# A four-layer convolution and attention kernel: ScalarE issues two of the eight row gathers of v per step, and VectorE sums the two heads ahead of the residual

## The chip, the cores and the metric

The kernel runs on one core of one Trainium2 chip. The metric is the time of one execution on the device in microseconds (us); the value quoted for a kernel is the median of its runs. A core has five engines that work from instruction queues of their own: TensorE (PE, matrix products; PEld is its loading of weights), VectorE (DVE), ScalarE (ACT), GpSimd (POOL) and SyncE (SP, which here only starts DMA transfers). Each engine executes its queue in the order in which it was written; engines wait for each other by semaphores.

## The reference, cut to what matters

Four residual layers are computed on x of shape (8, 128, 56, 56), all in float32: window attention, a recurrent network, a masked convolution and a pair of 3x3 convolutions. The change touches only the first. For each of 8 images, with 7 x 7 windows of 64 pixels, 8 heads of 16 channels, and for each window the 4 windows that its mean query likes best:

```python
xn = group_norm(x)                                  # 32 groups of 4 channels
q, k, v = xn @ W_qkv + b_qkv                        # per pixel, 128 channels each
_, r_idx = top_k(q_win * 128**-0.5 @ k_win.T, 4)    # 4 of 49 windows, for each window
attn = softmax(q_h * 128**-0.5 @ k_h[r_idx].T)      # 8 heads, 64 queries x 256 keys
o = attn @ v_h[r_idx]
x = x + (o + depthwise3x3(v) + lepe_b) @ W_o + b_o
```

## The kernel before, in words

Layer 0 is a software pipeline over 196 pairs of windows (8 images x 49 windows, two at a time). One pass of its last loop is called a step here. In step `p` the engines work on several pairs at once: `gather` (L487) copies the chosen keys of pair p+3 on POOL; `fetch` (L505) starts the DMA transfers that bring the chosen rows of v of pair p+2; `scores` (L524) multiplies queries and keys of pair p+2 on PE, and `maxima` (L539, four instructions max0 to max3) takes their row maxima on DVE; `halve`, `flip` and `flipped` bring these maxima onto the right partitions (POOL, PE, ACT); `shifted` (L560) computes the transposed and shifted scores of pair p+1 on PE; `exponentials` (L583, four instructions exp0 to exp3) takes their exponentials on ACT; and `values` (L589) multiplies exponentials and rows of v of pair p on PE into the PSUM tile `po`.

The results of a head pair lie in two halves of `po`, which have to be masked and added. `first_heads` (L607) scales the first half on ACT into `v`, and `both_heads` (L612, instruction L615) adds the second half to it on DVE. `divisors` (L617) prepares the divisors on DVE, and `divide` (L633) multiplies on POOL.

Beside this a planner gives most steps one or two further jobs, called `one` and `two`, each a product on PE and an ending (`end1`, `end2`) on ACT or DVE: keys, queries, pixels or rows of v for the next image (endings on ACT), the depthwise convolution (24 matmuls, L420, ending on ACT), or `project` (L439), the output projection. The ending of `project` is the residual, L450 on DVE, which adds the projection (PSUM) to X. There are 56 of them, one per strip of 7 windows. `hooks` are small loose pieces of work, most of them statistics on DVE.

The order of the work within a step is written out by hand: two strings list the names, SHORT for most steps, LONGER for those with a depthwise convolution, and in these strings lies the order on each of PE, ACT, DVE and POOL. SP is not bound by it, but takes its transfers in the order of their making.

PSUM tiles are shared, and this ties the engines to each other. `po` lies in the same bank (s0) as a quarter of the scores: the scores of the next pair can begin only after `both_heads` has read `po`, and `values` only after max0 has read its scores. `one` uses bank t0, `two` t1 and `flip` t2, which `shifted` also writes and exp0, exp1 and exp2 read.

The rows of v lie in DRAM as `vpix`, one block of 64 pixels x 128 channels (32 KB) per window. A pair needs eight of them (2 windows x 4 chosen). They go to `ring`, which has room for 6 windows, that is three pairs. In `fetch`, ScalarE's queue issues the first (o = 0, t = 0) and SP's queue the other seven. Before `values` of a pair, PE waits on the two semaphores `landed` of its windows (L594). Which window is chosen is known only at run time: `chosen` (L474) loads the indices into registers of the issuing engine (TENSOR_LOAD at L470), for SP and POOL four windows at a time, for ScalarE the index t = 0 of every second of seven windows, so four values and one load for about four steps.

Of the kernel before, what the change touches and what calls it, by code (L numbers as in the profile page):

```python
# [26 lines left out]
NWIN = NW * NW  # L27
# [3 lines left out]
TOPK = 4  # L31
# [15 lines left out]
def conv_stack_kernel(ctx: ExitStack, tc: tile.TileContext, a: dict, out: bass.AP):  # L47
# [3 lines left out]
    nc = tc.nc  # L51
# [76 lines left out]
    with ExitStack() as l0:  # L128
# [41 lines left out]
        for i in range(2):  # L170
            t = c0.tile([P, WS, PW], F32, name=f"vrow{i}", tag=f"vrow{i}")
# [10 lines left out]
        qs, ks, selrs, v3s, lepes, os_, st1, norms = {}, {}, {}, {}, {}, {}, {}, {}  # L182
        later, tails = [], []
# [281 lines left out]
        known = {}  # L465
        landed = [tc.alloc_semaphore(f"landed{k}") for k in range(RING)]

        def loaded(src, engine):

            return nc.values_load_multi_w_load_instructions(  # L470
                src, engines=[engine], min_val=0, max_val=NWIN - 1,
                skip_runtime_bounds_check_because="indices of maxima over 49 values, clamped to 48",
            )[1]

        def chosen(W, t, engine):

            if (engine, W, t) not in known:
                b, w = divmod(W, NWIN)
                if engine == mybir.EngineType.Activation:
                    at = selrs[b].rearrange("p (w t) -> p w t", t=TOPK)[:, w : min(w + 7, NWIN) : 2, t]  # L480
                    known.update(((engine, W + 2 * k, t), v) for k, v in enumerate(loaded(at, engine)))
                else:
                    vs = loaded(selrs[b][0:1, w * TOPK : min(w + 4, NWIN) * TOPK], engine)
                    known.update(((engine, W + k // TOPK, k % TOPK), v) for k, v in enumerate(vs))
            return known[engine, W, t]

        def gather(W):  # L487


            for W in (W, W + 1):  # L490
                b, w = divmod(W, NWIN)
                i, j = divmod(w, NW)
                kw = win.tile([P, TOPK, WPX], F32, name=f"ks_{W}", tag="ks", bufs=5)
                for t in range(TOPK):
                    at = chosen(W, t, mybir.EngineType.Pool)
                    nc.gpsimd.tensor_copy(kw[:, t : t + 1, :], ks[b][:, bass.ds(at, 1), :])  # L496
                qm = win.tile([P, 2, WPX], F32, name=f"qm_{W}", tag="qm", bufs=5)
                nc.gpsimd.tensor_tensor(
                    qm, qs[b, i][:, j : j + 1, :].broadcast_to((P, 2, WPX)),
                    hmask.rearrange("p (h o) -> p h o", o=1).broadcast_to((P, 2, WPX)), ALU.mult,  # L500
                )
                wins[W] = dict(kw=kw.rearrange("p t x -> p (t x)"), qm=qm)

        def section(W, c):
            return 4 * (W % RING) + 2 * c + 1  # L505

        def fetch(W):

            for o in range(2):
                for t in range(TOPK):  # L510
                    h = (t % 2) * WPX
                    engine, kind = (nc.sync, mybir.EngineType.SP) if o or t else (
                        nc.scalar, mybir.EngineType.Activation)
                    at = chosen(W + o, t, kind)
                    dma = engine.dma_start(
                        ring[h : h + WPX, section(W + o, t // 2), :],
                        vpix[(W + o) // NWIN][bass.ds(at, 1)].rearrange("o x c -> (o x) c"),
                    )
                    dma.then_inc(landed[(W + o) % RING], 16)
                    tc.no_tile_sem_insts.add(dma.ins.name)  # L520
                    tc.add_to_no_dep_group(f"rows{W + o}", dma.ins)
# [33 lines left out]
        def flipped(p):  # L555
            t = pairs[p]["nm"] = win.tile([P, 2, P], BF16, name=f"nm_{p}", tag="nm", bufs=1)
            nc.scalar.copy(t, pairs[p]["flip"])
# [54 lines left out]
        def both_heads(p):  # L612

            s_ = pairs[p]
            nc.vector.scalar_tensor_tensor(s_["v"], s_["po"][:, :, 1], hmask[:, 1:2], s_["v"], ALU.mult, ALU.add)  # L615

        def divisors(p):  # L617


            s_ = pairs[p]  # L620
            t = win.tile([P, 2, 2, 2, CL], F32, name=f"den_{p}", tag="den", bufs=1)
            nc.vector.transpose(
                t.rearrange("p o h b r -> p (o h b r)"), s_["po"].rearrange("p o h q -> p (o h q)")
            )
            at = t[:, 0, 0, 0, 16:17]
            den = bass.AP(at.tensor, at.offset, [list(at.ap[0]), [4 * CL, 2], [CL, 2], [2 * CL - 16, 2]])
            rden = win.tile([P, 2, 2, 2, 1], F32, name=f"rden_{p}", tag="rden", bufs=1)
            nc.vector.reciprocal(rden.rearrange("p o b h c -> p o b (h c)"), den)
            s_["d"] = win.tile([P, 2, WPX], F32, name=f"d_{p}", tag="d", bufs=1)
            nc.vector.transpose(  # L630
                s_["d"].rearrange("p o (k r) -> p (o k) r", r=CL),
                rden.rearrange("p o b h c -> p (o b) h c").broadcast_to((P, 4, 2, 16)),
            )  # L633

        def divide(p):

            s_ = pairs.pop(p)
            for o in range(2):
                W = 2 * p + o
                b, w = divmod(W, NWIN)  # L640
                i, j = divmod(w, NW)
                if j == 0:
                    os_[b, i] = strip.tile([P, WS, HW], F32, name=f"o_{b}_{i}", tag="o")
                n = 2 if o == 0 and j + 1 < NW else 1
                if o == 1 and j > 0:
                    continue
                dst = os_[b, i][:, :, j * WS : (j + n) * WS]
                nc.gpsimd.tensor_tensor(
                    dst.rearrange("p u (o v) -> p o u v", v=WS),
                    s_["v"][:, o : o + n].rearrange("p o (u v) -> p o u v", v=WS),  # L650
                    s_["d"][:, o : o + n].rearrange("p o (u v) -> p o u v", v=WS), ALU.mult,
                )
# [12 lines left out]
        made, jobs, hooks, fixed, loose = {}, [], {}, [], []  # L665
# [14 lines left out]
        def pair_of(b, w):  # L680
            return (b * NWIN + w) // 2
# [40 lines left out]
        for f in (image[0], image[1], *pixels[1:]):  # L722
# [3 lines left out]
                     light=(ps_s, "s2"), tails=(ps_s, "s1"))  # L726
# [19 lines left out]
        for b in range(1, B):  # L746

            at = [FIRST + 1] * NBLK if b == 1 else [pair_of(b - 2, 0) + 2 * i - 1 for i in range(NBLK)]
# [9 lines left out]
            at = [pair_of(b - 1, i * NW) - 5 for i in range(NBLK)]  # L758
            if b == 1:
                at = [max(t, 4 + 3 * i // 2) for i, t in enumerate(at)]  # L760
# [16 lines left out]
        for p in range(FIRST, END + 6):  # L777
            ready = [t for t in jobs if t[1] <= p and all(placed.get(k, p) < p for k in t[7])]
            light, long = (next((t for t in ready if t[5] == k), None) for k in (LIGHT, LONG))
            ready = [t for t in ready if t[5] == ONE]  # L780
            one = next((t for t in ready if not t[4]), None)
            if long:
                one, two = one if len(ready) > (MANY if p > 20 else 8) else None, long
# [3 lines left out]
            if light and two and two[4] and p < light[0]:  # L787
                light = None
# [9 lines left out]
        for b, i in itertools.product(range(B), range(NBLK)):  # L798
            p = placed["project", b, i]
# [5 lines left out]
        for lo, hi, n, f in sorted(loose, key=lambda t: t[0]):  # L805
            p = min(range(lo, min(hi, END + 5) + 1), key=lambda p: (weight[p], p))
# [21 lines left out]
        for k, (name, n) in enumerate(VECTORS):  # L828
# [4 lines left out]


        SHORT = """fetch scores shifted gather max0 max1 values exp0 max2 exp1 max3 halve ahead one light two flip exp2
            divisors first end1 exp3 flipped both divide lit hooks tails end2"""
        LONGER = """fetch scores shifted gather max0 max1 values exp0 max2 exp1 max3 halve ahead two exp2 divisors first
            flip light one exp3 flipped both divide lit hooks tails end2 end1"""

        def ahead(p):  # L840
            for W in (2 * p - 2, 2 * p - 1):
# [19 lines left out]
        for p in range(FIRST, END + 6):  # L861
            one, two, light = (t and t[3]() for t in plan[p])
# [3 lines left out]
            if 0 <= p + 2 < END:  # L866
                acts.update(scores=lambda: scores(p + 2), halve=lambda: halve(p + 2), flip=lambda: flip(p + 2),
                            flipped=lambda: flipped(p + 2))
# [6 lines left out]
            if 0 <= p < END:  # L875
                acts.update(values=lambda: values(p), first=lambda: (first_heads(p), root_table(p)),
                            both=lambda: both_heads(p), divisors=lambda: divisors(p), divide=lambda: divide(p))
            if p >= 0 and p + 2 < END:
                acts["fetch"] = lambda: fetch(2 * p + 4)
# [13 lines left out]
            for W in (0, 2) if p == -1 else ():  # L893
                fetch(W)
# [11 lines left out]
    with ExitStack() as l1:  # L906
# [5 lines left out]
        at = np.cumsum([0] + [n for _, n in VECTORS])  # L912
# [18 lines left out]
        t = c1.tile([P, B], F32, name="t1")  # L931
# [154 lines left out]
        with tc.manual_schedule(engines={mybir.EngineType.PE}):  # L1086
# [3 lines left out]
            for s in range(0, END, 2):  # L1090
# [22 lines left out]
                if s + 2 == WARM:  # L1113
                    first = [row.tile([P, 2, 2, NCH, B], F32, name=f"first{f}", tag=f"hs{f}", bufs=3) for f in range(2)]
# [10 lines left out]
        known = st2[:, : len(tiles), :]  # L1125
# [762 lines left out]
```

## Time and profile before

| | us |
|---|---|
| median of 3 timed runs | 3370.28 (3366.54 to 3371.79) |
| the profiled execution, whole | 3365.47 |
| its span, first to last instruction | 3363.6 |
| TensorE busy in it | 3246.4 (97%) |
| VectorE busy | 1767.8 (53%) |
| ScalarE busy | 1412.6 (42%) |
| GpSimd busy | 1291.8 (38%) |

Layer 0 covers about the first 1190 us: the 196 steps are marked by the 196 transposes of `divisors` (L622), the first at 50.9 us and the last at 1187.9 us. In a row of the timeline the first number is the start, the second the duration, both in us; then come engine, line, operation, tiles (written, then read), shapes and a count; in brackets stands how long the engine had been idle before it and what ended that. "SPq" and "ACTq" are the queues of SP and ScalarE when they issue a transfer, which does not count as busy time. The granted clock of TensorE was 0.988 over the span.

### The profile page before, as it was taken

How to read it: one execution, taken by the hardware profiler on the slowest of the kernel's cores; microseconds unless marked ns; L12 is line 12 of the kernel's file. 1: busy time of each engine (PE TensorE's matmuls, PEld its weight loads, DVE VectorE, ACT ScalarE, POOL GpSimd, SP SyncE). 2: the span in 40 equal slices, each digit the busy share in tenths (PEclk: the TensorE clock that was granted, in tenths of full speed). 3: DMA queues.
4: the chain of work that ended last, by engine and by line, in shares of the span. 5: the costliest groups of instructions: out<-in, count | busy, mean ns of one | idle time of the engine just before them, and what ended most of it. 6: DMA issues, size and time to landing. Idle time of an engine off the chain costs nothing.

```text
span 3363.6 us, 103407 instructions
## 1 busy us (share of the span) xinstructions
PE 3246.4 (97%) x41152; PEld 2743.4 (82%) x41152; DVE 1767.8 (53%) x4066; ACT 1412.6 (42%) x2935; POOL 1291.8 (38%) x3797
## 2 busy tenths in 40 slices
PE   7999999999999899999999999999999999999998
PEld 5777767667676689999999999999999953489898
DVE  5888888788776732221111111111122247799999
ACT  4666666566665522222222222222211144455554
POOL 4777877877777721111111111111000046422221
PEclk9999999999999989999999999999999999999999
DMA  5455555545445411110000000000012146301001
GB/s 152 132 142 134 146 142 134 138 124 143 124 129 140 112 58 45 48 48 18 1 1 1 1 1 1 1 1 1 1 51 60 57 122 181 94 20 39 27 32 40
DMA packets 197564, 239.02 MB, mean 71 GB/s; under 512 B 42848, under 2 KB 150112, under 8 KB 197072
## 3 DMA queue, kind: packets, MB, share of 16 engines
q0 software_dynamic: 34624, 117.03, 12.7%
q1 hardware_dynamic: 145936, 108.38, 11.3%
q10 hardware_dynamic: 16512, 6.90, 0.9%
q8 instruction: 326, 5.34, 0.7%
q14 instruction: 166, 1.36, 0.1%
HBM read 133.64 MB, written 67.56 MB: 60 GB/s over the span
## 4 chain that ended last, share of the span: by engine, by line
PE 75%; DVE 18%; issue 3%; POOL 1%; ACT 1%; DMA 1%; SPq 0%; POOLq 0%; DVEq 0%; ACTq 0%
PE ps L1041 35%; PE s L534 6%; PE po L600 6%; PE po L1076 5%; PE plep L420 4%; PE pc L1267 4%; PE t L576 4%; DVE nmax L541 3%; PE pi L1016 3%; PE t L566 1%; PE pc L1275 1%; DVE u_pc3b L1632 1%; PE pq L390 1%; PE pvp L319 1%; DVE va L1499 1%
## 5 line engine op out<-in xcount | busy, mean ns | idle before, releaser
L1041 PE MATMUL ps<-hs,w_gates 128*128 128x136 f32 x7680 | 932.9, 280 | 0.4 <-issue 0.4
L1041 PEld LDWEIGHTS ps<-hs,w_gates 128*128 128x128 f32 x7680 | 911.1, 190 | 8.6 <-issue 0.5
L1064 ACT ACTIVATE hs<-ps,bg 128x136 f32<-128x136 f32 x744 | 237.9, 371 | 933.1 <-PE ps L1041 925.6
L586 ACT ACTIVATE e<-t 128x512 f32<-128x512 f32 x784 | 445.6, 595 | 345.3 <-PE t L576 273.6
L541 DVE TENSOR_REDUCE nmax<-s 128x2 f32<-128x512 f32 x784 | 487.0, 685 | 196.4 <-PE s L534 195.6
L1019 DVE SCALAR_TENSOR_TENSOR inp<-pi,bine,th 128x272 f32<-128x272 f32 x186 | 84.7, 496 | 889.2 <-ACT th L1018 889.2
L1005 POOL TENSOR_TENSOR xn<-X,ctr 128x136 f32<-128x136 f32 (+1 forms) x186 | 96.3, 536 | 876.4 <-PE pi L1016 871.6
L1041 PEld LDWEIGHTS ps<-inp,w_gates 128*128 128x128 f32 x2976 | 370.2, 190 | 13.5 <-PE pi L1016 1.1
L1041 PE MATMUL ps<-inp,w_gates 128*128 128x136 f32 x2976 | 375.4, 279 | 0.7 <-PE pi L1016 0.7
L496 POOL COPY ks<-kT 128x64 f32 x1568 | 297.0, 234 | 106.2 <-PE t L576 64.8
L600 PE MATMUL po<-e,ring 128*32 128x64 f32 x12544 | 247.2, 231 | 24.7 <-DVE nmax L541 17.9
L600 PEld LDWEIGHTS po<-e,ring 128*32 128x32 f32 x12544 | 220.0, 149 | 49.6 <-DVE nmax L541 20.1
L534 PE MATMUL s<-ks,qm 32*128 32x256 f32 x3136 | 228.4, 403 | 19.0 <-DVE v L615 15.2
L576 PE MATMUL t<-qm,ks 32*128 32x128 f32 x6272 | 235.6, 273 | 0.6 <-issue 0.6
L576 PEld LDWEIGHTS t<-qm,ks 32*128 32x128 f32 x6272 | 216.5, 188 | 4.8 <-issue 1.4
L1513 PE MATMUL pc3b<-vb,u_w2c_t 128*128 128x196 f32 x1152 | 200.9, 336 | 19.9 <-DVE vb L1494 19.9
L1513 PEld LDWEIGHTS pc3b<-vb,u_w2c_t 128*128 128x128 f32 x1152 | 197.3, 194 | 22.2 <-DVE vb L1494 22.0
L1076 PE MATMUL po<-hs,xw 128*128 128x272 f32 x744 | 203.9, 396 | 3.4
L1513 PE MATMUL pc3a<-va,u_w1c_t 128*128 128x196 f32 x1152 | 198.2, 332 | 9.1 <-DVE d_pc3a L1530 4.3
L1513 PEld LDWEIGHTS pc3a<-va,u_w1c_t 128*128 128x128 f32 x1152 | 192.9, 191 | 13.6 <-issue 10.2
L534 PEld LDWEIGHTS s<-ks,qm 32*128 32x128 f32 x3136 | 144.6, 185 | 50.1 <-DVE v L615 27.4
L1076 PEld LDWEIGHTS po<-hs,xw 128*128 128x128 f32 x744 | 132.0, 190 | 28.8 <-ACT hs L1068 9.1
(288 smaller groups left out, 4410.7 us busy)
## 6 DMA issues: line engine op xcount, KB each, us to landing
ring<-vpix SPq DMA_DIRECT2D x1372, 32.0 KB
v<-vimg POOLq DMA_DIRECT2D x56, 290.0 KB, 3.9
v<-vimg POOLq DMA_DIRECT2D x56, 289.5 KB, 4.8
v<-vimg POOLq DMA_DIRECT2D x56, 289.0 KB, 5.7
kept<-gk SPq DMA_DIRECT2D x56, 272.0 KB, 2.0
g<-kept SPq DMA_DIRECT2D x56, 272.0 KB, 2.6
xkeep<-X POOLq DMA_DIRECT2D x56, 224.0 KB, 2.5
vimg<-vrow POOLq DMA_DIRECT2D x54, 232.0 KB, 2.8
```

Of the source, the lines that this page charges most:

```text
L420: nc.tensor.matmul(st["pl"][g * CL : (g + 1) * CL], wlep[:, dy, g, :], rows[:, g, dy : dy + WS, :HW], start=(dy == 0), stop=(dy == 2),)
L496: nc.gpsimd.tensor_copy(kw[:, t : t + 1, :], ks[b][:, bass.ds(at, 1), :])
L534: nc.tensor.matmul(s_["s"][g][:, o, :], w["qm"][h].rearrange("p h x -> p (h x)"), w["kw"][h], start=True, stop=True,)
L541: nc.vector.tensor_reduce(s_["nmax"][:, :, g], s_["s"][g], AX.X, ALU.max, negate=True)
L576: nc.tensor.matmul(s_["t"][g][:, o, c], w["kw"][h, c * P : (c + 1) * P], w["qm"][h].rearrange("p h x -> p (h x)"), start=False, stop=(o == ...
L586: nc.scalar.activation(s_["e"][g], s_["t"][g], AF.Exp)
L600: mm = nc.tensor.matmul(po[g * CL : (g + 1) * CL, o, h], flat[:, at : at + 8 * CL - 7 : 8], s_["e"][g][:, o, c, h * WPX : (h + 1) * WPX], ...
L1041: nc.tensor.matmul(ps[f][:, i], w, src, start=(i == 0 and k == 0 and h != fresh), stop=(k == KH - 1 if h else k == KI - 1 and (s < WARM or ...
L1064: nc.scalar.activation(hs[f][:, s % 2, i], ps[f][:, i], AF.Tanh, bias=bg[:, m : m + 1])
L1076: nc.tensor.matmul(po, wout[:, k, :], hs[k // 2][:, :, k % 2], start=(k == 0), stop=(k == KH - 1))
L1267: nc.tensor.matmul(pcs[n][r * CL : (r + 1) * CL], w3[:, dy, r, :], rows3[:, r, i * WS + dy : i * WS + dy + WS, :HW], start=(dy == 0), stop ...
L1513: nc.tensor.matmul(bank[:, half].rearrange("p (y x) -> p y x", x=H4), u[:, dy, k, :], v[:, k, i * RB + dy : i * RB + dy + RB, :], start=(d ...
```

## The change

In `fetch` ScalarE issues the gather t = 0 of both windows of a pair, so two, and SP six. For that ScalarE's load takes the index t = 0 of eight windows in a row in place of every second of seven. In both lists of names `both` moves: in SHORT to between `first` and `end1`, ahead of the residual where `one` is a projection; in LONGER to right behind `first`, where nothing of DVE stands between the old and the new place except for the endings that follow later anyway.

```diff
@@ chosen
                 if engine == mybir.EngineType.Activation:
-                    at = selrs[b].rearrange("p (w t) -> p w t", t=TOPK)[:, w : min(w + 7, NWIN) : 2, t]
-                    known.update(((engine, W + 2 * k, t), v) for k, v in enumerate(loaded(at, engine)))
+                    at = selrs[b].rearrange("p (w t) -> p w t", t=TOPK)[:, w : min(w + 8, NWIN), t]
+                    known.update(((engine, W + k, t), v) for k, v in enumerate(loaded(at, engine)))
@@ fetch
-                    engine, kind = (nc.sync, mybir.EngineType.SP) if o or t else (
+                    engine, kind = (nc.sync, mybir.EngineType.SP) if t else (
                         nc.scalar, mybir.EngineType.Activation)
@@ the order of a step
         SHORT = """fetch scores shifted gather max0 max1 values exp0 max2 exp1 max3 halve ahead one light two flip exp2
-            divisors first end1 exp3 flipped both divide lit hooks tails end2"""
+            divisors first both end1 exp3 flipped divide lit hooks tails end2"""
         LONGER = """fetch scores shifted gather max0 max1 values exp0 max2 exp1 max3 halve ahead two exp2 divisors first
-            flip light one exp3 flipped both divide lit hooks tails end2 end1"""
+            both flip light one exp3 flipped divide lit hooks tails end2 end1"""
```

## The prediction

> **What bounds the kernel now.** I read the page for the share of each engine, then the views of one line (L622, L515) for the rhythm, then the waits of PE, then the timeline of three stretches. Layer 0 is the only part that the change touches.
>
> ```profile
> PE 3246.4 (97%) x41152; PEld 2743.4 (82%) x41152; DVE 1767.8 (53%) x4066; ACT 1412.6 (42%) x2935; POOL 1291.8 (38%) x3797
> ```
> ```profile
> L622 DVE STREAM_TRANSPOSE den<-po x196: 427/450/452, 50.9 to 1187.9; 128x256 f32<-128x256 f32 x196
> ```
> ```profile
> L515 SPq DMA_DIRECT2D ring<-vpix x1372: 468/468/1777, 32.9 to 1183.0; - x196
> L515 ACTq DMA_DIRECT2D ring<-vpix x196: 476/482/548, 44.7 to 1172.3; - x196
> ```
> ```profile
> 164.69 139.22 SPq L515 DMA_DIRECT2D ring<-vpix  x168
> ```
>
> PE is the engine that is nearly always busy. The 196 marks of L622 lie (1187.9 - 50.9) / 195 = 5.83 us apart: that is a step. A second queue has no air either: SP issued 168 gathers, the share of 24 steps, in 139.22 us, or 5.80 us a step, without a pause in the timeline. An issue takes 468 ns, but with its register work and the index loads between them they follow at 0.83 us, and some take up to 1777 ns. SP starts about three pairs ahead and loses this lead: counted in the trace, from SP's last issue for a pair to PE's use of the pair 10 to 15 us pass in the first ten steps and 2 to 5 us in the last fifteen. So two things are near the limit: PE with what it waits for, and SP.
>
> ```profile
> PE s L534 <- DVE v L615: 15.0, 41, 1.0
> ...
> PE po L600 <- DMA ring<-vpix: 4.1, 1, 4.1
> ```
> ```profile
> 1049.38 0.31 DVE L630 STREAM_TRANSPOSE d<-rden 128x128 f32<-128x128 f32 x1
> ...
> 1049.61 0.65 DVE L450 SCALAR_TENSOR_TENSOR X<-py,bo,X 128x448 f32<-128x448 f32 x1
> ...
> 1050.04 0.28 PE L553 MATMUL flip<-ident,halves 128*128 128x128 bf16 x2
> ...
> 1050.17 0.34 DVE L615 SCALAR_TENSOR_TENSOR v<-po,hmask,v 128x128 f32<-128x128 f32 x1
> ...
> 1050.57 1.15 PE L534 MATMUL s<-ks,qm 32*128 32x256 f32 x16 [0.26 <-DVE v L615]
> ...
> 1056.96 1.30 PE L600 MATMUL po<-e,ring 128*32 128x64 f32 x40 [4.13 <-DMA ring<-vpix]
> ```
>
> This is a step with a residual. PE is through with the flip at 1050.32 and stands 0.26 us, because the scores need the PSUM bank that L615 has yet to read, and L615 stood behind the residual. The last line is PE waiting 4.13 us for gathered rows.
>
> **The change part by part.**
>
> (1) *The sum ahead of the residual.* Before, L615 starts 0.56 us after L450 (1049.61 to 1050.17). Without L450 ahead it starts where L450 starts now, its inputs being there (the halves of ScalarE end 0.1 to 0.2 us before the divisors in nearly all steps). Nothing else on DVE moves; behind L615 wait L450 and the hooks, and they end when they end now. What PE gets depends on its own work, by classes counted over the trace:
> - 20 steps with the projection and an image row (L301) as second job: PE idles 0.27 us on average; the next exp0 has 0.22 us to spare against ScalarE's ending of that job. Gain 0.225 x 20 = 4.5.
> - 7 with the projection and queries (L390): 0.26 idle, 0.27 to spare. 0.25 x 7 = 1.75.
> - 12 with pixels (L319): 0.12 idle. 0.12 x 12 = 1.4.
> - 5 with the projection alone: about 1.0 idle; the scores can start 0.57 earlier. 0.57 x 5 = 2.85.
> - Of the rest some 0.3 in all; where a depthwise convolution is beside it, nothing moves on DVE.
>
> Sum 10.8 us. What is late next: L450 ends 0.3 us later against the scores, while `shifted`, which overwrites its PSUM bank, comes 0.97 us after the start of the scores and the residual needs 0.31 + 0.65 from the same point: it just fits. Max0 has DVE idle for 0.3 to 1.2 us before it in these steps, more than the scores come earlier. Without this cover the 10.8 shrink towards 0.
>
> (2) *One gather less on SP.* Six at 0.83 are 4.97 us in a step of 5.83, so the lead is kept. Then the stalls on rows go: 4.13 us (above) and, in the last fifteen steps, where PE starts 0.13 us after the landing, 0.25 + 0.34 + 0.23 + 1.52 = 2.3 us. Sum 6.4. It is also what lets part (1) count: at 5.80 of 5.83 a faster PE would only wait for SP. On SP everything behind the moved gather comes earlier, with one exception: by the order of the changed program both weight loads for layer 1 (1.0 and 0.5 MB) now stand directly ahead of the same pair's gathers that stalled; before, one of them stood a pair earlier.
>
> (3) *One gather more on ScalarE.* It stands at the head of the step, ahead of exp0 to exp3; for them wait PE's jobs (through the banks), `first_heads`, the flip's copy and the ending of `two`, which PE's `shifted` needs.
>
> ```profile
> 805.23 0.52 ACTq L515 DMA_DIRECT2D ring<-vpix  x1
> ...
> 805.99 1.09 ACT L586 ACTIVATE e<-t 128x512 f32<-128x512 f32 x2 [1.25 <-PE t L576]
> ...
> 809.46 0.48 ACTq L515 DMA_DIRECT2D ring<-vpix  x1
> 809.57 0.61 ACT L338 COPY vp<-pvp 128x512 f32<-128x512 f32 x1
> ...
> 811.42 1.09 ACT L586 ACTIVATE e<-t 128x512 f32<-128x512 f32 x2 [1.25 <-PE t L576]
> ```
>
> A further gather costs about 0.65 us of the queue: at the start three of them take 1.86. The second case is the ordinary one: the issue ends at 809.94, exp0 starts when PE releases it at 811.42, and 1.48 us lie between; 0.65 of it costs nothing. The first is a step with an index load (median 920 ns) ahead of the gather: 0.24 us lie between. Counted over the trace 42 steps have less than 0.65, and their shortfalls add up to 16.8 us with the usual 0.05 between issue and exp0. That is the upper bound of the cost; the lower is 0. Of each shortfall the 0.24 us that exp2 waits for `values` anyway swallow a part; with a depthwise convolution next, exp1 has 0.15 to spare, and the idle time before the flip's copy (0.4 to 1.2) takes more. Step by step that leaves 2.0 in ordinary steps, 2.2 in residual steps and 1.9 in those with the convolution: I take 6.1. The new loads (56 for 52) shift by one step for every second image, to like places.
>
> (4) *The beginning.* The first pair's second gather now waits for ScalarE, which issues it 0.65 us after the first (44.66, 45.3), while SP had issued it by 37.5. PE waits for exactly this landing at 48.87. Cost 0.65.
>
> Sum: -10.8 - 6.4 + 6.1 + 0.65 = -10.5 us. The profiled execution took 3365.47 (span 3363.6 and 1.9 around it), so 3355.0 by its measure. It stands 4.8 under the median of the runs, 3370.28; measured like that median the forecast is 3359.8.
>
> A rule that speaks against this: the Trainium skill, "DMA: Bandwidth & Descriptors", section "Issuing engines are not separate DMA queues", says that transfers started from several engines share the same 16 DMA engines, and that this only saves sequencer time, usually little beside the transfer. By it the 6.4 us of part (2) would stay, and the sum would be -4.1. The row on SP says that here sequencer time is what has run out, while the DMA engines are busy about half the time (share 0.52 from 100 to 300 us): by it the sum is -10.5.
>
> **The rivals.**
> - *ScalarE's lateness eats the gain* (0.15). For: the 42 tight steps; in 104 steps the flip's copy has idle time before it, in the rest none. Against: the spare times in (3). With all 16.8: -17.2 + 16.8 + 0.65 = +0.3, so 3370.5.
> - *The rows land late all the same* (0.10), because the transfers collide (gathers landing 4 to 5 us after their issue occur where 870 KB for the convolution or the layer 1 weights are under way). Then (2) gives nothing: -4.1, so 3366.2. This is also the case in which that half of the change does not do what it says.
> - *More than I count* (0.12). ScalarE's lateness is swallowed whole: -16.6, so 3353.7.
> - *Slower* (0.13). The second issue on ScalarE, right behind the first, is not 0.48 us long but slow, as SP's are when several are under way (up to 1.78; 8% of them over 1.0). In the 50 steps with an index load there is no cover left, so each 0.1 us of it costs 5 us; from 0.2 us it has eaten the gain, from 0.34 the kernel is measurably slower. With 0.5: +25 - 10.5 = +14.5, so 3384.8. Against: ScalarE's own issues never took over 0.55, but then it had one at a time.
>
> **How the numbers follow.** Forecast -10.5: 3359.8, chance 0.50, own range 3355.7 to 3363.5 (ScalarE's cost 2 to 10 in place of 6.1). 0.2% is 6.7 us, about what a measurement of this kernel can tell from no change; the bound lies at 3363.5. Faster: forecast and "more than I count", 0.62. Within: the first two rivals, 0.25. Slower: 0.13. The range for 8 in 10 goes from 3351 (just under the 3353.7) to 3374 (the first two rivals, and a second issue slow by up to a quarter us); beyond it I leave the rest of the slower case and a little below.
>
> **What would show it.** In the changed profile: L615 ahead of L450 in the residual steps, and the wait of scores on L615 down from 15.0 us to about 3; SP's gathers at 1176 with pauses between groups of six; no wait of L600 on the ring behind the first step; ScalarE's issues at 392, of 0.48 us each; exp0 late by up to 0.6 us every fourth step and in no others; the marks of L622 about 10 us closer in all. I am wrong if exp0 comes late in ordinary steps too, if the pair behind the weight loads still stalls by 4 us, or if the waits on L615 turn into equal ones on L450 (by `shifted`) or on max0 (by `values`).

## The result

The changed kernel is slower. Its median is 3389.43 us (3380.94 to 3393.65, 6 runs), that of the kernel before on the same chip 3368.41 us (3362.79 to 3371.79, 6 runs): a ratio of 1.0063, with an interval from 1.0047 to 1.008, or 21 us more. The forecast was 3359.8, with a range of 3351 to 3374: wrong in sign, and outside the range.

### The profile page after: what moved, and what is told of

The parts are those of the page before. It is cut to its first block, busy times and chain, and to the rows that moved or that the text cites. A ratio compares the mean times of both kernels' runs of the same rounds, so it can differ in the third digit from the quotient of the medians.

```text
span 3391.6 us, 103411 instructions
## 1 busy us (share of the span) xinstructions
PE 3249.3 (96%) x41152; PEld 2737.9 (81%) x41152; DVE 1776.9 (52%) x4066; ACT 1400.1 (41%) x2935; POOL 1292.9 (38%) x3797
## 4 chain that ended last, share of the span: by engine, by line
PE 76%; DVE 14%; issue 4%; ACT 2%; ACTq 2%; POOL 1%; DMA 1%; SPq 0%; DVEq 0%; POOLq 0%
PE ps L1041 35%; PE po L1076 5%; PE po L600 5%; PE s L534 5%; PE plep L420 4%; PE t L576 4%; PE pc L1267 4%; PE pi L1016 3%; PE t L566 2%; PE py L445 1%; ACTq L515 1%; PE pq L390 1%; PE pvp L319 1%; PE pc L1275 1%; PE pc3b L1513 1%
## 5 line engine op out<-in xcount | busy, mean ns | idle before, releaser
L586 ACT ACTIVATE e<-t 128x512 f32<-128x512 f32 x784 | 441.2, 596 | 377.5 <-PE t L576 203.2
L600 PE MATMUL po<-e,ring 128*32 128x64 f32 x12544 | 245.5, 230 | 16.8 <-DVE nmax L541 13.3
L600 PEld LDWEIGHTS po<-e,ring 128*32 128x32 f32 x12544 | 218.4, 149 | 41.6 <-DVE nmax L541 14.9
L420 PE MATMUL plep<-v,wlep 96*32 96x448 f32 x1344 | 140.3, 550 | 20.0 <-ACT e L586 20.0
```

The source lines that it names most:

```text
L420: nc.tensor.matmul(st["pl"][g * CL : (g + 1) * CL], wlep[:, dy, g, :], rows[:, g, dy : dy + WS, :HW], start=(dy == 0), stop=(dy == 2),)
L586: nc.scalar.activation(s_["e"][g], s_["t"][g], AF.Exp)
L600: mm = nc.tensor.matmul(po[g * CL : (g + 1) * CL, o, h], flat[:, at : at + 8 * CL - 7 : 8], s_["e"][g][:, o, c, h * WPX : (h + 1) * WPX], ...
```

## The profile after

The profiled execution took 3393.65 us, with a span of 3391.6. First the shares of the engines on its page, then the rhythm of the steps (L622: count, shortest, median and longest in ns, first and last start in us).

```profile
PE 3249.3 (96%) x41152; PEld 2737.9 (81%) x41152; DVE 1776.9 (52%) x4066; ACT 1400.1 (41%) x2935; POOL 1292.9 (38%) x3797
```
```profile
L622 DVE STREAM_TRANSPOSE den<-po x196: 427/450/452, 51.6 to 1213.1; 128x256 f32<-128x256 f32 x196
```

PE has as much work as before, but the step is now (1213.1 - 51.6) / 195 = 5.96 us long instead of 5.83. So PE waits more: 25 of the 28 us by which the span grew have come by the end of layer 0. The granted clock (0.99) is no lower than before. The waits of PE between 60 and 1215 us say for whom (us in total, times, longest):

```profile
PE plep L420 <- ACT e L586: 20.0, 16, 2.3
PE po L600 <- DVE nmax L541: 13.3, 8, 2.6
PE pq L390 <- ACT e L586: 10.7, 16, 1.2
...
PE py L445 <- ACT e L586: 4.9, 8, 1.2
PE s L534 <- DVE v L615: 4.3, 12, 0.4
...
PE pvp L319 <- ACT e L586: 2.9, 7, 0.4
```

Two of the intended effects are there: the wait of the scores on L615 fell from 15.0 us to 4.3, and there is no wait of L600 on the ring any more. But four rows are new. The jobs `one` and `two` (L420, L390, L445, L319) wait for the exponentials of L586, which have yet to read the banks that the jobs write: 20.0 + 10.7 + 4.9 + 2.9 = 38.5 us. Before, these jobs waited for them 0.2 us in all. So ScalarE is late. What it does ahead of its exponentials shows in the timeline of one step:

```profile
801.03 0.38 ACT L557 COPY nm<-flip 128x256 bf16<-128x256 bf16 x1
801.15 0.48 ACTq L515 DMA_DIRECT2D ring<-vpix  x1
801.28 0.72 ACT L307 ACTIVATE vrow<-pvt,bqkv 128x448 f32<-128x448 f32 x1
...
803.27 1.24 PE L600 MATMUL po<-e,ring 128*32 128x64 f32 x64
...
803.86 0.50 ACTq L515 DMA_DIRECT2D ring<-vpix  x1
...
804.41 1.57 ACT L586 ACTIVATE e<-t 128x512 f32<-128x512 f32 x3 [2.41 <-PE po L600]
...
805.55 2.46 PE L420 MATMUL plep<-v,wlep 96*32 96x448 f32 x24 [1.04 <-ACT e L586]
```

ScalarE's first gather is issued by 801.63, the second only at 803.86. Between them the timeline shows nothing for ScalarE, because a load into registers does not count as work; in the trace it stands there from 801.66 to 803.67. Exp0 should start where `values` (L600) starts, at 803.27. It starts at 804.41, right behind the second gather and 1.14 us late, and L420 waits 1.04 us for the exponentials. The bracket behind L586 names PE as what ended the idle time; that is only the last event the profile knows of. In the trace it lies at 804.04, and the last product of `shifted`, which exp0 reads, had ended at 803.34. What exp0 waited for stood ahead of it in its own queue.

The load has a row of its own in the view of L470 (shortest, median and longest in ns). Of the kernel before:

```profile
L470 ACTq TENSOR_LOAD <-selr x52: 284/920/1822, 43.2 to 1155.4; - x52
```
And after:
```profile
L470 SPq TENSOR_LOAD <-selr x104: 302/976/1708, 29.9 to 1201.8; - x104
L470 ACTq TENSOR_LOAD <-selr x56: 282/1733/2364, 44.6 to 1202.2; - x56
```

ScalarE's load has doubled, from 0.92 to 1.73 us, as it takes eight values where it took four. (SP takes sixteen in 0.98 us, but its sixteen are neighbours in the list, while ScalarE's are every fourth.) Counted over the trace, exp0 starts 1.16 us after the start of `values` on average in the 52 steps with a load. What goes beyond 0.05 us in a step adds up to 58.0 us; before it was 1.3 us. In the other steps nothing changed (0.9 us against 1.3).

By an account of PE over layer 0, from the first `values` to the last (1138.9 us before, 1162.8 after, so +23.9): the four waits for exponentials +39, the scores' wait on L615 -12, waits of `values` -8, idle time ahead of `flip` and `shifted` +3, the products themselves +2. The layer also starts 1.4 us later.

## Experiments

Three explanations were set against each other. **L**: the index load, now 1.73 us and with a second gather behind it, no longer fits into the time that ScalarE has ahead of exp0. **I**: the second issue of a gather on ScalarE is itself what makes it late (the last rival of the prediction). **O**: the new order of the sum harms. Each kernel is compared with the kernel before on its own chip, where that took 3377.8, 3378.9 and 3375.4 us in the three groups; a difference in us is the measured ratio applied to that time, so it can be off by 1 to 2 us from the difference of the medians. "Lateness" is the sum over the steps with a load of what exp0 starts more than 0.05 us after `values`, counted in the trace.

### The order alone

```diff
# before, with nothing but the two strings changed:
-            divisors first end1 exp3 flipped both divide lit hooks tails end2"""
+            divisors first both end1 exp3 flipped divide lit hooks tails end2"""
-            flip light one exp3 flipped both divide lit hooks tails end2 end1"""
+            both flip light one exp3 flipped divide lit hooks tails end2 end1"""
```


> Only the two lists of names are changed: the sum of the heads stands ahead of the residual, the gathers and ScalarE's index load are as before. Theory L (the changed kernel is slow because its index load on ScalarE, eight values that lie four apart, lasts 1.73 us in place of 0.9 and holds back the exponentials): nothing of that is here, so this is not slower than before. The wait of the scores on L615 falls from 15.0 us to about 4, and the time by 2 to 11 us: less than 10.8 if SP, which needs 5.80 of a step's 5.83 us, takes over as the limit; then waits for gathered rows grow. Theory O (the order itself does harm, by a residual that now comes late): slower by 5 us or more.

Measured: 3375.18 us, ratio 0.9992 [0.9981, 1.0004], no difference. PE's first waits between 60 and 1215 us:

```profile
PE po L600 <- DMA ring<-vpix: 18.4, 12, 4.2
PE po L600 <- DVE nmax L541: 15.5, 11, 2.6
PE s L534 <- DVE v L615: 4.7, 13, 0.4
```

The wait on L615 has fallen to 4.7 us, but the layer is as long as in the execution of before that was profiled later (1150.9 us both, though on different chips). By an account of PE in these two, the scores' idle time is 12 us less; about 5 us of it come back as idle time ahead of L600, where the waits on gathered rows are 18.4 us in place of 14.7, 6 us in the first products of `shifted` (see part (1) below), and the rest is spread. So SP takes back a part of the gain and `shifted` another. O falls: nothing here is slower.

### Gathers moved, with neighbouring indices

```diff
 (before's order; SP also copies the indices t = 0 of an image into a row of their own)
+                sel0s[b] = samp.tile([1, NWIN], I32, name=f"sel0_{b}", tag="sel0")
+                nc.sync.dma_start(sel0s[b], sel[:, 0:1])
...
+                    at = sel0s[b][0:1, w : min(w + 8, NWIN)]
...
-                    engine, kind = (nc.sync, mybir.EngineType.SP) if o or t else (
+                    engine, kind = (nc.sync, mybir.EngineType.SP) if t else (
```


> Only the gathers are changed: ScalarE issues two and SP six, the lists of names are as before, and ScalarE's indices come from a row of their own in which the choices t = 0 of an image's windows lie side by side (one more tiny transfer per image), so that it loads eight neighbouring values. Theory L: the load lasts about 0.5 us (SP's load of 16 neighbours lasts 0.97, of 4 neighbours 0.30), the exponentials are hardly late, and the waits for rows (6.4 us) go: 4 to 7 us faster than before. Theory I (it is the second issue on ScalarE that holds the exponentials back, whatever the load): 15 us slower or more.

Measured: 3360.36 us, ratio 0.9949 [0.9936, 0.9962], 17 us faster and more than any theory had. The load takes 0.55 us, lateness is 4.2 us. The second issues are as irregular as in the changed kernel (0.64 us on average, 21 over 1 us, the longest 2.0), and they cost nothing that can be seen. I falls.

### The whole change, with neighbouring indices

```diff
 (the changed kernel with the row of indices above)
-                    at = selrs[b].rearrange("p (w t) -> p w t", t=TOPK)[:, w : min(w + 8, NWIN), t]
+                    at = sel0s[b][0:1, w : min(w + 8, NWIN)]
```


> The whole change, with ScalarE's indices from the row of neighbouring values. Theory L: load about 0.5 us, so the whole of the gains that were forecast and little of the cost: 10 to 17 us faster than before, and the waits of PE's jobs on the exponentials (38 us in the changed kernel) gone to under 5. Theory I: 15 us slower or more than before, as the changed kernel.

Measured: 3350.01 us, ratio 0.9921 [0.9908, 0.9935], 27 us faster than before, and more than the 10 to 17 that L expected. Its load, and PE's first waits between 60 and 1215 us (its lines are numbered 3 higher):

```profile
L473 ACTq TENSOR_LOAD <-sel x56: 290/551/1099, 45.6 to 1159.0; - x56
```
```profile
PE po L603 <- DVE nmax L544: 13.9, 9, 2.7
PE s L537 <- DVE v L618: 5.3, 16, 0.5
PE flip L556 <- POOL halves L551: 3.9, 5, 1.1
```

Neither a wait for exponentials of any size nor one on the ring is left. A step with a load in the timeline, to be laid beside that of the changed kernel:

```profile
796.25 0.48 ACTq L518 DMA_DIRECT2D ring<-vpix  x1
796.36 0.59 ACT L339 COPY vp<-pvp 128x512 f32<-128x512 f32 x1
...
797.51 0.49 ACTq L518 DMA_DIRECT2D ring<-vpix  x1
...
798.20 1.09 ACT L589 ACTIVATE e<-t 128x512 f32<-128x512 f32 x2 [1.25 <-PE t L579]
```

The load (796.76 to 797.31 in the trace) stands at the same place, between the two gathers. The second gather ends at 798.00, and exp0 starts at 798.20, with `values` at 798.21: now it really is PE that releases it, with 0.2 us to spare. So one array's layout decides the sign of the whole change: 56 loads of 0.55 us instead of 1.73.

### The long load with one gather

```diff
 (before, ScalarE still issuing one gather; only the load takes all eight windows)
-                    at = selrs[b].rearrange("p (w t) -> p w t", t=TOPK)[:, w : min(w + 7, NWIN) : 2, t]
-                    known.update(((engine, W + 2 * k, t), v) for k, v in enumerate(loaded(at, engine)))
+                    at = selrs[b].rearrange("p (w t) -> p w t", t=TOPK)[:, w : min(w + 8, NWIN), t]
+                    known.update(((engine, W + k, t), v) for k, v in enumerate(loaded(at, engine)))
```


> The kernel before, with one thing of the change: ScalarE loads the indices t = 0 of eight windows in a row (four of them are not used), but still issues one gather. Theory L: the load lasts 1.73 in place of 0.9 us; of that the room before the exponentials hides about half and the wait of the third exponential 0.24 more, so some 50 steps are later by 0.2 to 0.4 us: 6 to 20 us slower than before. Theory I: no difference (within 3 us), since the second issue is not there.

Measured: 3381.71 us, ratio 1.0006 [0.9994, 1.0019], no difference: a miss for L's number, and what theory I expected (which fell with the two kernels above, and would not have with this one alone). The load is 1.83 us and lateness 22.9 us, but PE waits for exponentials only 7 us, and its waits on the ring come to 10.9 us (14.7 in the execution of before profiled below). That would fit a late PE giving time to SP, which this kernel waits for anyway; no run isolates it. What is shown is that the long load costs what it does only together with the second gather.

### The long load and both gathers, in before's order

```diff
 (the changed kernel with before's two strings)
-            divisors first both end1 exp3 flipped divide lit hooks tails end2"""
+            divisors first end1 exp3 flipped both divide lit hooks tails end2"""
```


> Before's order of the names, but the second gather on ScalarE and its index load of eight values 16 bytes apart, as in the changed kernel. My theory (the index load of 1.73 us ahead of two gathers makes exp0 late in every fourth step, some 55 us of lateness in all, of which PE waits for e about 38): slower than before by 5 to 32 us; exp0 late by 45 to 65 us in sum over the steps with a load, and PE's waits on e of L586 25 to 45 us. The rival that the new order of the sum harms, together with the load: no slower than before, with PE's waits on e below 10 us. The rival that a second gather alone is too slow for ScalarE has already fallen with the run of neighbouring indices.

Measured: 3391.51 us, ratio 1.004 [1.0025, 1.0055], 13 us slower; lateness 52.8 us, waits for exponentials 15.0 + 10.5 + 5.9 + 2.9 = 34.3 us. This half of the change carries the loss by itself.

### The changed kernel with shorter loads

```diff
 (the changed kernel; first kernel)
-                    at = selrs[b].rearrange("p (w t) -> p w t", t=TOPK)[:, w : min(w + 8, NWIN), t]
+                    at = selrs[b].rearrange("p (w t) -> p w t", t=TOPK)[:, w : min(w + 2, NWIN), t]
 (second kernel: min(w + 4, NWIN))
```


> The whole change, but ScalarE loads two indices (16 bytes apart) every second step in place of eight every eighth window: a load of about 0.45 us in place of 1.73, in nearly every step. My theory (what costs is how much longer than the room of some 1.5 us between two gathers' end and PE's release the load and the second gather together are in one step): 0.45 + 0.65 fits, so a time near that of the kernel with neighbouring indices, faster than before by 17 to 28 us; exp0's lateness below 12 us in sum. The rival that the sum of what ScalarE spends on indices counts, however it is cut (196 x 0.45 = 88 us against 56 x 1.73 = 97): slower than before by 10 to 20 us, like the changed kernel.

> The whole change with loads of four indices 16 bytes apart, in every second step: 0.9 us each, the length that the forecast gave the load. My theory: with 0.65 for the second gather and 0.05 between, 0.9 + 0.65 is just over the room of 1.48 us less what the ordinary step has spare; exp0 is late by 0.1 to 0.5 us in some 100 steps, most of it swallowed: faster than before by 10 to 24 us, between the kernel with neighbouring indices and the changed one, and nearer the former. The rival (the sum of time spent on loads): slower by 5 to 20 us, as 104 x 0.9 = 94 us are spent, as many as in the changed kernel.

Measured: with two values 3348.76 us, ratio 0.9916 [0.9901, 0.9931], 28 us faster than before; with four 3358.64 us, ratio 0.9944 [0.9929, 0.996], 19 us faster. Their loads:

```profile
L470 ACTq TENSOR_LOAD <-selr x200: 282/482/894, 44.4 to 1158.8; - x100
```
```profile
L470 ACTq TENSOR_LOAD <-selr x104: 281/894/1592, 44.5 to 1166.9; - x104
```

Added up in the traces, the 200 loads take 104 us and the 104 loads 95 us, no less than the 56 loads of the changed kernel (92 us). Still the time goes from -28 over -19 to slower than before, and lateness from 5.0 over 21.9 to 58.0 us. What counts is not the time spent on indices, but by how much a single load with its gathers is longer than the room in its step.

### Before once more, profiled

> The kernel before, profiled once more, on the same chip as the three others. If the stalls on the gathered rows are what the moved gather was worth more than 6.4 us for, PE's waits of L600 on the ring are 10 to 25 us here and not 6.4; if they are 6.4 again, the gain of the moved gather must have come from somewhere else.

Measured: 3377.64 us, with PE's first waits

```profile
PE s L534 <- DVE v L615: 15.7, 42, 1.0
PE po L600 <- DMA ring<-vpix: 14.7, 9, 3.4
```

The wait on L615 is that of the first execution, that on the ring is not: 14.7 us in nine waits instead of 4.1 in one. The layer is 12 us longer (1150.9 against 1138.9). Seen from here the 17 us of the moved gather are explained in the main, as that kernel has no such wait; they were small in the prediction because the execution it was read from had few stalls. On the chip where the moved gather was measured, before itself was timed but not profiled.

### The changed kernel once more, and the distance of the indices

```diff
 (against the whole change with neighbouring indices: the row now holds the first two choices of each window, values 8 bytes apart)
-                nc.sync.dma_start(sel0s[b], sel[:, 0:1])
+                nc.sync.dma_start(sel0s[b], sel[:, 0:2])
...
-                    at = sel0s[b][0:1, w : min(w + 8, NWIN)]
+                    at = sel0s[b].rearrange("p (w t) -> p w t", t=2)[:, w : min(w + 8, NWIN), t]
```


> The changed kernel once more, beside the repaired ones on their chip, since before took 3368 on the first chip and 3378 on the others, where it stalls more on gathered rows. The changed kernel has no such stalls, so its own time should not depend on the chip: 3381 to 3394 again, slower than before by 5 to 25 us, and at least 25 us slower than the kernel with neighbouring indices. If it were at or below before, the first comparison would have been one of chips.

> The whole change with ScalarE's eight indices 8 bytes apart (a row of the first two choices of each window) in place of 16 (the changed kernel: 1.72 us a load) or 4 (neighbours: 0.55). If a load costs some 0.21 us for each value that has no neighbour beside it in the list, 1.7 us, and a time like that of the changed kernel, +5 to +25 us against before. If it costs that much for each stretch of 16 bytes that it touches (eight values in 64 bytes, four stretches), 0.9 to 1.1 us, exp0 late by 10 to 25 us in sum, and faster than before by 10 to 24 us.

Measured: the changed kernel 3388.82 us, ratio 1.0044 [1.0027, 1.0061]; with values 8 bytes apart 3388.76 us, ratio 1.0041 [1.0027, 1.0056]. The changed kernel takes the same time on both chips, and is slower on both; what differs is before, with its stalls. The load 8 bytes apart:

```profile
L473 ACTq TENSOR_LOAD <-sel x56: 280/1732/2583, 43.0 to 1197.0; - x56
```

It takes the 1.73 us of 16 bytes apart, and lateness is the same too (57.2 us in the changed kernel, 55.2 here). Whether lone values lie 8 or 16 bytes apart doesn't matter; being neighbours does.

### A third gather on ScalarE

```diff
 (neighbouring indices, eight in every second step; ScalarE issues t = 0 of both windows and t = 1 of the first)
-                    engine, kind = (nc.sync, mybir.EngineType.SP) if t else (
+                    engine, kind = (nc.sync, mybir.EngineType.SP) if t > (o == 0) else (
```


> Three of the eight gathers on ScalarE, five on SP; ScalarE loads eight neighbouring indices every second step (0.55 us). My theory: SP's lead is already 12 us with six gathers, so a fifth of its work less brings nothing more, while 0.55 + 2 x 0.65 = 1.85 us no longer fit in the 1.48 us of room; exp0 late by 25 to 45 us in sum over the steps with a load and by a few us in the others: 8 to 35 us slower than the kernel with two gathers and neighbouring indices, so -20 to +8 against before. The rival that SP still bounds with six gathers: as fast as that kernel or faster, -27 to -40.

Measured: 3382.17 us, ratio 1.0023 [1.0013, 1.0032], 8 us slower than before and so some 34 slower than with two gathers. Lateness is 54.1 us, above the 25 to 45 that were expected. SP's lead was already enough, and this time the room was filled by gathers instead of by the load.

## Why the prediction was wrong

**The step that failed is in part (3)**: "The new loads (56 for 52) shift by one step for every second image, to like places." The places were right, the length was not. The load was carried over with the 0.92 us of the old one, though the diff beside it took eight values in place of four; nothing in the sum had a term for a longer load. By the prediction's own arithmetic the right length gives the loss: 0.24 us were left in a load step, the load grew by 0.81 and a gather costs 0.65, so exp0 comes 0.65 + 0.81 - 0.24 = 1.22 us late, in 52 steps 63 us; measured 58.0. PE pays 38.5 of it where the forecast had 6.1. The bound of 16.8 us was worked out from the same short load, so the range was too narrow as well: an "upper" bound holds only for the terms in it.

A price was to be had on both sides. The row of SP's load gave sixteen values in 0.97 us; the Trainium skill, "Runtime: NRT & Kernel Launch", section "Instruction fetch mechanics", says that a register load takes about 200 ns for each register, even for many at once, and speaks there of the loads in a kernel's preamble. ScalarE's rows here agree with it (0.28 us for one value, 0.92 for four, 1.73 for eight); the row of SP and the load of eight neighbours in 0.55 us do not, and there the rows decide. Between 0.55 and 1.73 lay the sign of the result.

**Part (1)**, 10.8 us, came out in size where nothing else bounds: the whole change with neighbouring indices is 10 us faster than the same without the new order (3350.01 and 3360.36 us, same chip). Alone it brings nothing that can be measured, as the prediction said ("a faster PE would only wait for SP"), though by the account above SP took back only about 5 of the 12 us. In the kernel with both and neighbouring indices a residual step now reads

```profile
1028.46 0.31 DVE L618 SCALAR_TENSOR_TENSOR v<-po,hmask,v 128x128 f32<-128x128 f32 x1
...
1028.69 0.67 DVE L453 SCALAR_TENSOR_TENSOR X<-py,bo,X 128x448 f32<-128x448 f32 x1
1028.88 0.28 PE L556 MATMUL flip<-ident,halves 128*128 128x128 bf16 x2
...
1029.09 0.74 PEld L537 LDWEIGHTS s<-ks,qm 32*128 32x128 f32 x16
1029.09 1.15 PE L537 MATMUL s<-ks,qm 32*128 32x256 f32 x16
...
1029.52 0.69 ACT L308 ACTIVATE vrow<-pvt,bqkv 128x448 f32<-128x448 f32 x1
...
1030.06 0.60 PE L569 MATMUL t<-nm,ones 2*128 2x512 bf16 x4
```

with the scores right behind the flip and no wait in brackets. A part returns at another place: the first products of `shifted` (L566; here L569) take some 6 us more over the layer in every kernel with the new order. It is not the residual they wait for: in the kernel above that ends at least 0.17 us before `shifted` begins, so that the prediction's "it just fits" held. It is ScalarE. Of the four products the second starts 0.14 us after the first in a residual step, and 0.02 us without the new order; in 44 of 54 such steps it starts 0.05 us after ScalarE's ending of job `two` (L308 for an image row, L339 for pixels, L397 for queries), and without the new order in 5. In the step shown L308 ends at 1030.21, and the second product starts at 1030.27. The prediction checked that ending against the next exp0, but not against `shifted`, which comes earlier. So of some 11 us that the scores' wait loses here, nearly 7 come back; that the gain is 10 all the same, because other products take 5 us less, has no account and is in part luck.

**Part (2)** was right in kind and too small: 6.4 us foreseen, 17 measured. The term was read from one execution of before, with 4.1 us of waits on the ring in the view; others had 14.7 and, with the order alone, 18.4. Against its own execution the term was nearly right: the layer of the kernel with the gathers moved alone is 9 us shorter than there, 8 of them idle time ahead of L600. The prediction cited a warning that spreading transfers over engines saves only sequencer time, which is usually little (the Trainium skill, "DMA: Bandwidth & Descriptors", section "Issuing engines are not separate DMA queues"). Here it was not little: SP's queue, whose pauses over 0.2 us add up to 21 us between 60 and 1160 us of the kernel before, has 116 us of them with six gathers in the old order, and the waits on the ring are gone. Whether anything but sequencer time was saved no run shows. The weight loads for layer 1, which stood ahead of the gathers, caused no stall.

**Part (4)** can't be judged: `values` starts at 50.25 us after and at 48.87 before, but at 50.9 in the kernel with the order alone, whose gathers are before's.

**The rival on the other side** had the right place, the steps with a load, and the wrong cause. The second issue is indeed slower than the first (0.61 us on average against 0.49, 15 of 196 over 1 us, the longest 1.65), but the kernels with a short load have the same and lose nothing. That exp0 would be late "every fourth step and in no others" was right; the "up to 0.6 us" was 2.4.

## What to carry to other kernels

Where an edit changes how many values an instruction takes, price the instruction anew, above all one that is not counted as busy time: a register load stands in its engine's queue like anything else. Work that is put ahead of a timed instruction is free up to the room in that step and makes the instruction late beyond it (of 58 us of lateness PE paid 38.5 here), so cut it into pieces that fit (two values a step) or lay the data out so that it is short (a row of neighbours); either makes this change 27 to 28 us faster than before instead of 15 to 21 slower. And when two engines are near the limit together, an edit that relieves one may show its worth only beside an edit that relieves the other: the new order alone brought nothing that could be measured, and 10 us beside the moved gather, which was worth 17 us by itself.

## What the runs showed of the hardware

- What a register load takes depends on whether its values are neighbours in the list, not on their number alone. Medians on ScalarE: two values 16 bytes apart 0.48 us, four 0.89, eight 1.73; eight 8 bytes apart 1.73; eight neighbours 0.55. On SP sixteen neighbours take 0.97. So about 0.21 us for each lone value, and 0.06 to 0.07 for a neighbour, taken over the whole load.
- The stalls of the kernel before on gathered rows vary: 4.1 us in one profiled execution, 14.7 in another, and its medians from 3368 to 3379 us with them. The changed kernel, which has none, came out at 3389.4 and 3388.8 us on two chips. That SP's queue at its limit is what makes before differ fits, but is not shown: within one chip the changed kernel's times spread as widely (13 us against 9). One execution's stalls are a weak measure of what relieving a queue is worth.
